# Seven half-size products per part: the next part's transposes and sums in the first half of a part, and two places for those sums

## The chip, the cores and the metric

The kernel runs on one core of a Trainium2 chip. A core has a matrix engine (TensorE, PE in the profile; its weight loads are PEld), a vector engine (VectorE, DVE), an activation engine (ScalarE, ACT), GpSimd (POOL, which here issues the gathers and the adding writes), SyncE (SP, which issues the plain loads) and 16 DMA engines. The metric is device time in microseconds (us). Everything is in float32.

## The reference

A layer of attention and feed-forward is followed by a second one, whose last step is a mixture of experts. The change touches only that step:

```python
routing_weights = softmax(x2d @ gate_kernel)                 # 2048 tokens, 32 experts
routing_weights, selected = top_k(routing_weights, 8)
routing_weights = routing_weights / sum(routing_weights)
w0 = ragged_dot(sorted_inputs, gate_proj, group_sizes)       # 512 -> 192, each row by its expert
w1 = ragged_dot(sorted_inputs, up_proj, group_sizes)         # 512 -> 192
expert_out = ragged_dot(silu(w0) * w1, down_proj, group_sizes)   # 192 -> 512
output = sum over a token's 8 experts of routing_weight * expert_out
```

The tokens are 4 x 512 = 2048, the width is 512, and the hidden width of an expert is 192. The second layer's output is the input plus this sum.

## The kernel before

The experts are ranked by how many rows they got. Rank r has a fixed room of so many tiles of so many rows (`FIXED`: 7 tiles of 126 rows for the fullest, 2 tiles of 100 for the emptiest). `work` holds the 32 ranked experts in the order in which they are computed; an expert with more than four tiles is cut into two **parts** (7 tiles are 3 + 4, 6 are 3 + 3, 5 are 2 + 3), the others are one part. There are 46 parts. The main loop runs over them under a manual schedule: on TensorE, VectorE and ScalarE the instructions stand in the order in which the code issues them. The queues of POOL and SP are filled in the same course, with their own waits.

A part of n rows goes like this. Its gathered rows are transposed (`turn`: four chunks of 128 of the 512 columns; TensorE transposes L1374; three chunks are copied out by ScalarE, L1382, the fourth by VectorE, L1380). The hidden width of 192 is computed as three column groups of 128: gate 0 to 127, up 0 to 127, and one mixed group with the last 64 of gate and of up. The mixed group is a plain product of n columns (L1397), followed by `silu_half` (ScalarE L1198, two VectorE multiplications L1203). The first two groups are done either as plain products (L1397, with L1682 and L1686 after them) or by `Blocks.products` as **seven products of half the columns** (Strassen's scheme in Winograd's form): the weights are four blocks (gate1, gate2, up1, up2, by halves of the 512), the transposed rows four blocks (x11, x12, x21, x22, by halves of the 512 and halves of the rows). Four sums of weight blocks (s1 to s4, `weight_sums`, L1559 to L1562, once per expert) and four of row blocks (t1 to t4, `row_sums`, L1580 to L1584, once per part) are made on VectorE.

The text calls the products of a part, in TensorE's order:

- P1 = gate1·x11, P2 = gate2·x21, P3 = s2·t2, P4 = s1·t1, P5 = s4·x22, P6 = s3·t3, P7 = up2·t4 (all L1598, two matmuls each), and P8, the mixed group (L1397, four matmuls of n columns).

Between them VectorE adds (L1604): P1 + P2 (then SiLU into the low half of sg, L1609), u2 = P1 + P3, u4 = u2 + P4, u4 + P5 (then SiLU into the high half, L1617), u3 = u2 + P6, u3 + P4 (multiplied by sg into the high half of h1, L1621), u3 - P7 (into the low half, L1625). The products alternate between two pools of two PSUM banks each (`bank`); a product waits until the last reader of its bank is done.

`output` of a part is run inside the next part: the downs of a pair of tiles (L1209 and L1212, 512 columns), then the scaling by the routing weight (ScalarE L1485, for the second tile VectorE L1483), then the adding writes on POOL (L1413). A part of three or four tiles has two such groups, a part of two tiles one.

In the kernel before, the order within a part is: P1, P2; first group of downs; P3, P4; transposes of chunk 0 of the next part; P5; second group of downs; P6; chunk 1; P7; chunk 2; then t1 of the next part and, where a new expert follows, s1 to s4; P8 and `silu_half`; chunk 3; t2, t3, t4; the output weights of the next expert (L1440, L1443); the gathers of the expert three ahead (`more`, L916). The sums have one place: ws (s1 to s4) and us (P1, u2 to u4) share the tile big2, ts is in big0. The tiles big1 and big3 are idle in this stage once the early experts' rows, which lay in them, have been added.

The loads of an expert's weights (`fetch`: gu L908, d1 L909, d2 L910) and of its row list (L928) are in SP's queue; each waits until its buffer is free (three buffers).

Of the kernel before, what the change touches and what calls it, by code (L numbers as in the profile page):

```python
# [9 lines left out]
F32 = mybir.dt.float32  # L10
# [8 lines left out]
P = 128  # L19
# [4 lines left out]
EARLY = 6  # L24
# [26 lines left out]
def kernel(  # L51
# [26 lines left out]
    nc = tc.nc  # L78
# [3 lines left out]
    E, MI, _ = w_dn.shape  # L82
# [19 lines left out]
    big = ctx.enter_context(tc.tile_pool(name="big", bufs=1))  # L102
# [1219 lines left out]
    with tc.tile_pool(name="rw", bufs=1, reuse_waits="tile") as rw, tc.tile_pool(  # L1322
# [218 lines left out]
        class Blocks:  # L1541
# [3 lines left out]
            def __init__(self):  # L1545
                ws_us, ts = (
                    big.tile([P, 2048], F32, tag=f"big{i}", name=f"big{i}") for i in (2, 0)
                )
                ws_us = ws_us.rearrange("p (i m) -> p i m", i=8)
                self.ws = [ws_us[:, i, :].rearrange("p (k m) -> p k m", k=2) for i in range(4)]  # L1550
                self.us = [ws_us[:, 4 + i, :] for i in range(4)]
                ts = ts.rearrange("p (i k m) -> p i k m", i=4, k=2)
                self.ts = [ts[:, i, :, :] for i in range(4)]

            def weight_sums(self, gu):
                sub = ALU.subtract
                s1, s2, s3, s4 = self.ws
                gate1, gate2, up1, up2 = self.weights(gu)
                nc.vector.tensor_tensor(s1, up1, up2, ALU.add)  # L1559
                nc.vector.tensor_tensor(s2, s1, gate1, sub)  # L1560
                nc.vector.tensor_tensor(s3, gate1, up1, sub)
                nc.vector.tensor_tensor(s4, gate2, s2, sub)  # L1562

# [11 lines left out]
            def row_sums(self, xgt, n, first):  # L1575
                sub = ALU.subtract
                t1, t2, t3, t4 = (t[:, :, : n // 2] for t in self.ts)
                x11, x12, x21, x22 = self.blocks(xgt, n)
                if first:
                    nc.vector.tensor_tensor(t1, x12, x11, sub)  # L1580
                else:
                    nc.vector.tensor_tensor(t2, x22, t1, sub)
                    nc.vector.tensor_tensor(t3, x22, x12, sub)
                    nc.vector.tensor_tensor(t4, t2, x21, sub)  # L1584

            def products(self, gu, xgt, n, h1, sg, among):
                m = n // 2
                lo, hi = slice(0, m), slice(m, n)
                s1, s2, s3, s4 = self.ws
                t1, t2, t3, t4 = (t[:, :, :m] for t in self.ts)  # L1590
# [4 lines left out]
                def product(w, x):  # L1595
                    q = bank()
                    for k in range(2):
                        nc.tensor.matmul(  # L1598
                            q[:, :m], w[:, k, :], x[:, k, :], start=(k == 0), stop=(k == 1)
                        )  # L1600
                    return q[:, :m]

                def plus(out, a, b, op=ALU.add):
                    nc.vector.tensor_tensor(out, a, b, op)  # L1604

                nc.scalar.copy(p1, product(gate1, x11))
                q = product(gate2, x21)
# [3 lines left out]
                plus(u2, p1, product(s2, t2))  # L1611
                q22 = product(s1, t1)
# [32 lines left out]
        with tc.manual_schedule(engines=order):  # L1645
# [10 lines left out]
            outputs = iter(())  # L1656
            for i, (k, t0, nt) in enumerate(parts):
# [3 lines left out]
                after, todo, nxt = None, iter(()), None  # L1661
# [5 lines left out]
                by_seven = nxt is not None and n_nxt % 2 == 0  # L1667

                def step():
                    return next(todo, None)  # L1670

                places = iter((
                    lambda: next(outputs, None),
                    step,
                    lambda: next(outputs, None),
                    step,
                ))
                if i and n % 2 == 0:
                    seven.products(x.wt[0], xgt, n, h1, sg, lambda: next(places)())
                else:  # L1680
                    p = product(x.wt[0], xgt, 0, n)
                    nc.scalar.activation(sg[:, :n], p[:, :n], AF.Silu)  # L1682
                    next(places)()
                    p = product(x.wt[0], xgt, 1, n)
                    next(places)()
                    nc.vector.tensor_mul(h1[:, :n], p[:, :n], sg[:, :n])  # L1686
                    next(places)()
                    next(places)()
# [186 lines left out]
```

## Time and profile before

| | before |
|---|---|
| time, median of 3 runs | 1727.82 us (1725.8 to 1729.0) |
| the profiled execution | 1772.52 us |
| its span, first to last instruction | 1770.7 us |
| mean granted TensorE clock | 0.98 |
| stage of the ranked experts in it | about 1104 to 1758 us |
| instructions | 19464 |

The profile is of one execution, which took longer than the timed ones; sums are made within it. A line of a group or of the timeline names the source line, the engine, the operation and the tile that is written and those that are read ("g" is a bank of products, "tr" a bank of transposes, "dn" of downs, "xgt" transposed rows, "gu" an expert's gate and up weights, "big" the tiles of the sums). In the timeline the first two columns are start and duration in us; square brackets hold the idle time before an instruction and what ended it. A matmul in float32 appears as two records, so P1 is "x4".

### The profile page before, as it was taken

What the parts mean: (1) busy time and instruction counts of PE and PEld (TensorE: products, weight loads), DVE (VectorE), ACT (ScalarE), POOL (GpSimd) and SP (SyncE); (2) the same over time, 40 slices, a digit from 0 to 9 for tenths busy, and PEclk for the clock granted to TensorE, in tenths of its full rate; (3) what the DMA queues carried; (4) which work ended last, traced back from release to release, by engine and by line L of the source; (5) the groups of instructions that cost most, each with busy time, mean ns of one, the idle gap of its engine ahead of it and who ended that gap; (6) DMA issues with size and microseconds to landing.
All of it is one profiled execution on the core that took longest, in us unless ns stands there. A gap on an engine that the chain in (4) does not pass through costs nothing.

```text
span 1770.7 us, 19464 instructions
## 1 busy us (share of the span) xinstructions
PE 1662.0 (94%) x6530; PEld 1057.1 (60%) x6530; DVE 947.0 (53%) x2273; ACT 556.5 (31%) x993; POOL 600.1 (34%) x522
## 2 busy tenths in 40 slices
PE   7999999999999999999999779898999999999996
PEld 2784667776777677445445346565556666655553
DVE  4683467765775545444334226455255665565653
ACT  2510333322331111265556342232223232232331
POOL 1000130101100100113443646575556655555653
PEclk9999999999999999999999989999999999999998
DMA  9313140000000000722411226787677776687874
GB/s 347 112 60 107 48 175 25 1 1 1 1 0 24 0 1 1 251 101 94 139 51 47 71 89 173 187 157 153 147 165 173 171 152 149 154 176 183 178 151 52
DMA packets 94092, 188.88 MB, mean 107 GB/s; under 512 B 22016, under 2 KB 24704, under 8 KB 93990
## 3 DMA queue, kind: packets, MB, share of 16 engines
q0 software_dynamic: 40560, 74.02, 22.4%
q1 hardware_dynamic: 52564, 112.75, 19.0%
q8 instruction: 52, 0.85, 0.2%
q10 hardware_dynamic: 866, 0.85, 0.2%
q14 instruction: 50, 0.41, 0.1%
HBM read 133.46 MB, written 57.54 MB: 108 GB/s over the span
## 4 chain that ended last, share of the span: by engine, by line
PE 83%; DVE 6%; issue 4%; ACT 3%; DMA 2%; another core or an unknown queue 1%; POOL 0%; ACTq 0%; DVEq 0%; POOLq 0%
PE q L729 16%; PE dn L376 11%; PE g L1598 9%; PE g L1397 7%; PE dn L1209 7%; PE o L1030 6%; PE dn L1212 5%; PE sc L1000 5%; PE gu L354 5%; PE tr L1374 3%; PE g L1253 2%; PE tr L179 2%; DMA out_dram<-y,ids 1%; DVE h L1203 1%; DMA x_sb<-in_cn_dram 1%
## 5 line engine op out<-in xcount | busy, mean ns | idle before, releaser
L1413 POOL DMA_INDIRECT out_dram<-y,ids x141 | 226.1, 1604 | 149.5 <-ACT y L1485 89.2
L376 PE MATMUL dn<-wdn,h 128*128 128x512 f32 x448 | 200.3, 593 | 0.0
L1096 POOL DMA_INDIRECT il_d<-entry,slots x128 | 126.1, 985 | 206.6 <-DVE sel L1064 136.7
L916 POOL DMA_INDIRECT xg<-xn_d,ids x141 | 152.9, 1084 | 119.0 <-issue 60.4
L729 PE MATMUL q<-big,s 128*128 128x256 f32 x768 | 173.6, 379 | 0.0
L729 PEld LDWEIGHTS q<-big,s 128*128 128x128 f32 x768 | 145.9, 190 | 19.8
L1397 PE MATMUL g<-xgt,gu 128*128 128x351 f32 (+24 forms) x464 | 151.6, 470 | 2.2 <-DVE xgt L1380 2.2
L1209 PE MATMUL dn<-d,h 128*126 128x512 f32 (+8 forms) x306 | 148.4, 602 | 0.0
L376 PEld LDWEIGHTS dn<-wdn,h 128*128 128x128 f32 x448 | 84.1, 190 | 92.8 <-issue 91.6
L729 PE MATMUL q<-big,wgu 128*128 128x256 f32 x576 | 132.4, 379 | 0.0
L729 PEld LDWEIGHTS q<-big,wgu 128*128 128x128 f32 x576 | 109.3, 190 | 25.7 <-issue 9.3
L1030 PE MATMUL o<-big,pt 128*128 128x512 f32 x256 | 118.1, 610 | 3.8 <-ACT pt L182 2.0
L354 PE MATMUL gu<-big,wgu 128*128 128x256 f32 x512 | 118.0, 388 | 3.3 <-ACT sg L361 3.3
L1000 PE MATMUL sc<-big,qt 128*128 128x512 f32 x256 | 116.5, 609 | 0.3 <-ACT qt L182 0.3
L354 PEld LDWEIGHTS gu<-big,wgu 128*128 128x128 f32 x512 | 98.6, 194 | 26.6 <-issue 8.7
L1397 PEld LDWEIGHTS g<-xgt,gu 128*128 128x128 f32 x464 | 83.7, 192 | 47.6 <-issue 21.4
L386 POOL TENSOR_TENSOR x_sb<-x_sb,y 128x512 f32<-128x512 f32 x16 | 19.8, 1269 | 258.0 <-DVE y L385 258.0
L1598 PEld LDWEIGHTS g<-big,big 128*128 128x128 f32 x480 | 72.9, 190 | 57.2 <-issue 49.8
L290 POOL TENSOR_TENSOR x_sb<-x_sb,beta_t 128x512 f32<-128x512 f32 x16 | 23.8, 1509 | 236.7 <-ACT y L279 224.2
L1212 PE MATMUL dn<-d,h 64*126 64x512 f32 (+8 forms) x306 | 99.7, 641 | 0.2 <-DVE h L1203 0.2
L743 ACT ACTIVATE sg<-q,wsu_t 128x256 f32<-128x256 f32 x96 | 45.5, 474 | 171.4 <-DVE q L765 84.0
L1485 ACT ACTIVATE y<-dn,w 126x512 f32<-126x512 f32 (+8 forms) x95 | 63.9, 687 | 110.6 <-PE dn L1212 110.6
(273 smaller groups left out, 2560.5 us busy)
## 6 DMA issues: line engine op xcount, KB each, us to landing
gu<-in_w_gu_dram SPq DMA_DIRECT2D x38, 768.0 KB
big<-in_cn_dram SPq DMA_DIRECT2D x10, 1024.0 KB
d<-in_w_dn_dram SPq DMA_DIRECT2D x38, 256.0 KB
big<-in_ct_dram SPq DMA_DIRECT2D x8, 1024.0 KB
x_sb<-in_cn_dram SPq DMA_DIRECT2D x12, 512.0 KB
il_d<-x_sb SPq DMA_DIRECT2D x10, 512.0 KB
d<-in_w_dn_dram SPq DMA_DIRECT2D x38, 128.0 KB
xn_d<-xr SPq DMA_DIRECT2D x16, 272.0 KB
```

Source lines behind the costliest of these rows:

```text
L354: nc.tensor.matmul(ps[:, :n], wt[:, c, fs], xhs[b][:, c, cols], start=(c == 0), stop=(c == DC - 1),)
L376: nc.tensor.matmul(ps[:, :D], h[:, i * P : (i + 1) * P], wdn[:, fc, :], start=(fc == 0), stop=(fc == FC - 1),)
L729: nc.tensor.matmul(q[:, m * HS : (m + 1) * HS], w[:, m, k, :], x[:, k, :], start=(k == 0), stop=(k == 1),)
L916: ins = nc.gpsimd.indirect_dma_start(out=xg, out_offset=None, in_=src[:, :], in_offset=bass.IndirectOffsetOnAxis(ap=idx, axis=0), bounds_c ...
L1000: nc.tensor.matmul(ps[:, bass.ts(h, M // 2)], qt[:, c, :], keys[b][h][:, c, :], start=(c == 0), stop=(c == DC - 1),)
L1030: nc.tensor.matmul(ps[:, :D], pt[:, c, :], values[b][c // (MC // 2)][:, c % (MC // 2), :], start=(c == 0), stop=(c == MC - 1),)
L1096: ins = nc.gpsimd.indirect_dma_start(out=il_d[:, :], out_offset=bass.IndirectOffsetOnAxis(ap=slots[:, j : j + 1], axis=0), in_=entry, in_o ...
L1209: nc.tensor.matmul(p[:q, :D], h1[:, bass.ts(i, q)], d1, start=True, stop=False)
L1212: nc.tensor.matmul(p[:q, :D], h2[half, bass.ts(i, q)], d2[half, :], start=False, stop=True)
L1397: nc.tensor.matmul(p[:, :n], gu[:, c, m * P : (m + 1) * P], xgt[:, c, :n], start=(c == 0), stop=(c == DC - 1),)
L1413: ins = nc.gpsimd.indirect_dma_start(out=of[:, :], out_offset=bass.IndirectOffsetOnAxis(ap=idx, axis=0), in_=y, in_offset=None, bounds_che ...
L1598: nc.tensor.matmul(q[:, :m], w[:, k, :], x[:, k, :], start=(k == 0), stop=(k == 1))
```

## The change

`Blocks` gets two places each for the weight sums (in big2 and big3) and for the row sums (in big0 and big1), and takes them by turns, so the next part's sums can be written while the current ones are read. `row_sums` and `weight_sums` hand back the sums they wrote, and `products` is given them.

Within a part `among()` is called at six places instead of four. After P1: chunk 0 of the next part. After P2: chunk 1, then the first group of downs. After P3: chunk 2. After P4 (`last_turn`): chunk 3, then all four row sums, then the output weights if a new expert follows, then the gathers. After P5 and the adding to it (`next_weights`): the four weight sums if a new expert follows. After P6 and its two addings: the second group of downs. P7 and P8 follow without anything between. After P8 nothing is left of the next part's preparation, and its P1 comes next.

The seven products are now used only from the fourth part on (`i + 1 >= EARLY // 2` for the next part, with EARLY = 6), since the early experts' rows are still in big1 and big3 before that; the second and third part are done with plain products.

```diff
             def weight_sums(self, gu):
-                s1, s2, s3, s4 = self.ws
+                self.rooms_w = self.rooms_w[::-1]
+                s1, s2, s3, s4 = self.rooms_w[1]
...
-            def row_sums(self, xgt, n, first):
+            def row_sums(self, xgt, n):
-                t1, t2, t3, t4 = (t[:, :, : n // 2] for t in self.ts)
+                self.rooms_t = self.rooms_t[::-1]
+                sums = t1, t2, t3, t4 = [t[:, :, : n // 2] for t in self.rooms_t[1]]
                 x11, x12, x21, x22 = self.blocks(xgt, n)
-                if first:
-                    nc.vector.tensor_tensor(t1, x12, x11, sub)
-                else:
-                    nc.vector.tensor_tensor(t2, x22, t1, sub)
-                    nc.vector.tensor_tensor(t3, x22, x12, sub)
-                    nc.vector.tensor_tensor(t4, t2, x21, sub)
+                nc.vector.tensor_tensor(t1, x12, x11, sub)
+                nc.vector.tensor_tensor(t2, x22, t1, sub)
+                nc.vector.tensor_tensor(t3, x22, x12, sub)
+                nc.vector.tensor_tensor(t4, t2, x21, sub)
+                return sums
...
                 nc.scalar.copy(p1, product(gate1, x11))
+                among()
                 q = product(gate2, x21)
...
                 among()
                 plus(u2, p1, product(s2, t2))
+                among()
                 q22 = product(s1, t1)
...
+                seven_next = nxt is not None and n_nxt % 2 == 0 and i + 1 >= EARLY // 2
+
+                def turn_step():
+                    got["xgt"] = next(todo, None)
+
+                def last_turn():
+                    turn_step()
+                    if nxt is None:
+                        return
+                    if seven_next:
+                        got["x"] = seven.row_sums(got["xgt"], n_nxt)
+                    if after[1] == 0:
+                        got["w"] = nxt.weights()
+                    more(*after)
+
+                def next_weights():
+                    if seven_next and (after[1] == 0 or not by_seven):
+                        got["s"] = seven.weight_sums(nxt.wt[0])
+
                 places = iter((
+                    turn_step,
+                    lambda: (turn_step(), next(outputs, None)),
+                    turn_step,
+                    last_turn,
+                    next_weights,
                     lambda: next(outputs, None),
-                    step,
-                    lambda: next(outputs, None),
-                    step,
                 ))
...
-                following = step()
-                if by_seven:
-                    seven.row_sums(following, n_nxt, True)
-                    if after[1] == 0 or not (i and n % 2 == 0):
-                        seven.weight_sums(nxt.wt[0])
                 silu_half(product(x.wt[0], xgt, 2, n), h2, s2, nt, x.q)
-                step()
-                if by_seven:
-                    seven.row_sums(following, n_nxt, False)
                 outputs = output(x, t0, nt, h1, h2, w)
-                xgt = following
-                if nxt is not None:
-                    if after[1] == 0:
-                        w = nxt.weights()
-                    more(*after)
+                of_w, of_x, w, xgt = (got[v] for v in ("s", "x", "w", "xgt"))
```

More of the change, by code (lines that the diff above doesn't have):

```diff
@@ L1545, in __init__, with room, four @@
             def __init__(self):
[L1546 to L1553, printed above, removed]
+                def room(i):
+                    pool = big3 if i == 3 else big
+                    return pool.tile([P, 2048], F32, tag=f"big{i}", name=f"big{i}")
+                def four(v, w):
+                    v = v[:, : 4 * w].rearrange("p (i k m) -> p i k m", i=4, k=2)
+                    return [v[:, i, :, :] for i in range(4)]
+                rooms = [room(i) for i in (2, 0, 1, 3)]
+                self.us = [rooms[0][:, 1024 + i * 256 : 1280 + i * 256] for i in range(4)]
+                self.ws, self.ts = [], []
+                self.rooms_w = [four(rooms[i], 2 * P) for i in (0, 3)]
+                self.rooms_t = [four(rooms[i], 512) for i in (1, 2)]
             def weight_sums(self, gu):
                 sub = ALU.subtract
-                s1, s2, s3, s4 = self.ws
+                self.rooms_w = self.rooms_w[::-1]
+                s1, s2, s3, s4 = self.rooms_w[1]
                 gate1, gate2, up1, up2 = self.weights(gu)
@@ L1562, in weight_sums @@
                 nc.vector.tensor_tensor(s4, gate2, s2, sub)
+                return self.rooms_w[1]
             def weights(self, gu):
@@ L1573, in blocks, with products @@
                 ]
-            def row_sums(self, xgt, n, first):
+            def row_sums(self, xgt, n):
                 sub = ALU.subtract
-                t1, t2, t3, t4 = (t[:, :, : n // 2] for t in self.ts)
+                self.rooms_t = self.rooms_t[::-1]
+                sums = t1, t2, t3, t4 = [t[:, :, : n // 2] for t in self.rooms_t[1]]
                 x11, x12, x21, x22 = self.blocks(xgt, n)
-                if first:
-                    nc.vector.tensor_tensor(t1, x12, x11, sub)
-                else:
[L1582 to L1586, printed above, removed]
+                nc.vector.tensor_tensor(t1, x12, x11, sub)
[3 more added lines that the diff above has]
+                return sums
+            def products(self, gu, xgt, n, sums, h1, sg, among):
                 m = n // 2
                 lo, hi = slice(0, m), slice(m, n)
-                s1, s2, s3, s4 = self.ws
-                t1, t2, t3, t4 = (t[:, :, :m] for t in self.ts)
+                s1, s2, s3, s4, t1, t2, t3, t4 = sums
                 p1, u2, u3, u4 = (u[:, :m] for u in self.us)
@@ L1656 @@
             outputs = iter(())
+            of_w = of_x = None
             for i, (k, t0, nt) in enumerate(parts):
@@ L1660 @@
                 h1, h2, sg, s2 = hidden()
-                after, todo, nxt = None, iter(()), None
+                by_seven = of_x is not None
+                sums = by_seven and of_w + of_x
+                todo, after, nxt = iter(()), None, None
                 if i + 1 < len(parts):
@@ L1666, with among @@
                     n_nxt = after[2] * nxt.q
-                by_seven = nxt is not None and n_nxt % 2 == 0
-                def step():
-                    return next(todo, None)
-                places = iter((
+                seven_next = nxt is not None and n_nxt % 2 == 0 and i + 1 >= EARLY // 2
[13 more added lines that the diff above has]
+                        got["s"] = seven.weight_sums(nxt.wt[0])
+                got = {"s": of_w, "x": None, "w": w, "xgt": None}
+                places = iter((
+                    turn_step,
[3 more added lines that the diff above has]
+                    next_weights,
                     lambda: next(outputs, None),
-                    step,
-                    lambda: next(outputs, None),
-                    step,
-                ))
-                if i and n % 2 == 0:
-                    seven.products(x.wt[0], xgt, n, h1, sg, lambda: next(places)())
+                ))
+                def among():
+                    next(places)()
+                if by_seven:
+                    seven.products(x.wt[0], xgt, n, sums, h1, sg, among)
                 else:
@@ L1682 @@
                     nc.scalar.activation(sg[:, :n], p[:, :n], AF.Silu)
-                    next(places)()
+                    among()
+                    among()
                     p = product(x.wt[0], xgt, 1, n)
-                    next(places)()
                     nc.vector.tensor_mul(h1[:, :n], p[:, :n], sg[:, :n])
-                    next(places)()
-                    next(places)()
+                    for _ in range(4):
+                        among()
                 for _ in outputs:
```

## The prediction

> **What bounds the kernel now.** I read the busy times first, then who waited for whom on TensorE, then one part in order of time, then the granted clock after long waits. The busy line of the page:
>
> ```profile
> PE 1662.0 (94%) x6530; PEld 1057.1 (60%) x6530; DVE 947.0 (53%) x2273; ACT 556.5 (31%) x993; POOL 600.1 (34%) x522
> ```
>
> TensorE (PE) sets the time; VectorE (DVE) is half idle. Work comes off TensorE or a wait of it goes, or nothing is gained. Its waits in the stage of the ranked experts, 1104 to 1758 us (total, times, longest):
>
> ```profile
> PE g L1598 <- DVE xgt L1380: 28.1, 35, 3.1
> ...
> PE g L1598 <- issue: 1.9, 4, 0.5
> PE g L1598 <- DVE h L1203: 0.7, 1, 0.7
> ```
>
> These three are one wait: P2 of a part wants the fourth chunk of its own transposed rows, whose copy (L1380) stands behind the SiLU half (L1203) of the part before. 30.7 us over 40 parts. The longest, 3.1, came after ScalarE had started its SiLU 2 to 3 us late in this execution; its like elsewhere is 0.7. So **28.3 us** can be won.
>
> One part in order of time, with 3x126 rows (halves of 189 columns), the next part being 2x120 rows of another expert:
>
> ```profile
> 1418.38 0.37 PE L1374 MATMUL tr<-ident,xg 120*128 120x120 f32 x2
> ...
> 1418.58 0.35 DVE L1604 TENSOR_TENSOR big<-big,g 128x189 f32<-128x189 f32 x1 [0.29 <-PE g L1598]
> 1418.59 0.81 PE L1598 MATMUL g<-xgt,big 128*128 128x189 f32 x4
> ...
> 1419.23 0.80 PE L1598 MATMUL g<-big,big 128*128 128x189 f32 x4
> ...
> 1420.07 0.35 DVE L1604 TENSOR_TENSOR big<-big,g 128x189 f32<-128x189 f32 x1 [0.28 <-issue]
> ...
> 1421.85 0.40 DVE L1580 TENSOR_TENSOR big<-xgt 128x240 f32<-128x240 f32 x1
> 1422.17 0.42 DVE L1559 TENSOR_TENSOR big<-gu 128x256 f32<-128x256 f32 x1
> 1422.62 0.42 DVE L1560 TENSOR_TENSOR big<-big,gu 128x256 f32<-128x256 f32 x1
> 1422.96 0.42 DVE L1561 TENSOR_TENSOR big<-gu 128x256 f32<-128x256 f32 x1
> ...
> 1423.30 0.42 DVE L1562 TENSOR_TENSOR big<-gu,big 128x256 f32<-128x256 f32 x1
> ...
> 1425.02 0.41 DVE L1380 COPY xgt<-tr 128x240 f32<-128x240 f32 x1
> 1425.46 0.41 DVE L1582 TENSOR_TENSOR big<-xgt,big 128x240 f32<-128x240 f32 x1
> ...
> 1425.48 0.48 PE L1598 MATMUL g<-xgt,gu 128*128 128x120 f32 x2 [0.95 <-DVE xgt L1380]
> ...
> 1425.79 0.40 DVE L1583 TENSOR_TENSOR big<-xgt 128x240 f32<-128x240 f32 x1
> ...
> 1426.10 0.40 DVE L1584 TENSOR_TENSOR big<-big,xgt 128x240 f32<-128x240 f32 x1
> ...
> 1426.42 0.32 DVE L1440 TENSOR_TENSOR w<-xg,hot 120x160 f32<-120x160 f32 x1
> ...
> 1426.78 0.32 DVE L1443 TENSOR_REDUCE w<-w 120x5 f32<-120x160 f32 x1
> 1427.01 0.28 DVE L1604 TENSOR_TENSOR g<-big,g 128x120 f32<-128x120 f32 x1
> ```
>
> The reader should see where the sums lie: four of the weights (1422.17 on) under P8, which runs from 1420.94 for 2.71 us, and three of the rows under the first downs. TensorE waits for none of them.
>
> **What goes.** All 28.3 us: the fourth transposes, their copy and the sums are done well before the next part begins.
>
> **What comes: a chain on VectorE ahead of P8.** VectorE runs its instructions in program order. At the fourth place (between P4 and P5) it now gets the fourth copy, four row sums and the two instructions of the output weights; at the fifth (ahead of P6's adding) four weight sums where a new expert follows. Behind them stands u3 (L1604 after P6), the last reader of P6's bank, and P8 needs a bank. The trace tells which: P8 starts at 1420.94 while L1621, reader of P4's bank, runs from 1420.92 to 1421.27, so P8 doesn't wait for that one; the other bank of the pool is P6's, read by u3. In the kernel before u3 was always early. Now, for the part shown, from the start of its fourth transposes:
>
> - VectorE: u4 starts 0.20 after them (1418.38 to 1418.58) and takes 0.35, so the copy starts at 0.58; copy 0.39 (0.41 long; the next sum may start between 0.08 before its end and 0.04 after, I take 0.02 before); first row sum 0.43 (the second reads it), three more at 0.33 spacing 0.98; weights 0.59 (1426.42 to 1427.01); the adding after P5 0.28; weight sums 0.45 + 3 x 0.34 = 1.47; u3 0.35 and 0.06 to TensorE. Sum 5.13.
> - TensorE: transposes 0.21, P5, P6 and P7 0.64 each (1418.59 to 1419.23). Sum 2.13, as the part before has two tiles and leaves no downs for the sixth place. P8 waits **3.0**.
>
> By the same rows, with 0.55 for a row sum of 378 columns and 0.69 for 504, and the downs that fill the sixth place (2.01 for one tile, 1406.45 to 1408.46; 2.87 for two, 1401.82 to 1404.69), over the 37 parts of seven products that have a next part:
>
> - six with weight sums and no downs there (three-tile ends of five-tile experts): 3.0 each, 18.2
> - eight with weight sums and one tile: for 3x120 before 3x108, 5.41 against 4.17; mean 1.4, 11.1
> - eleven with weight sums and two tiles: for 4x126 before 4x126, 6.66 against 5.84, so 0.8; mean 0.6, 6.8
> - eight with row sums alone and one tile: 3.6 against 3.7, nothing; one with no tile, 1.5
> - three before an odd part, no sums: nothing.
>
> Together **37.6 us**. If each chain is 0.3 shorter it is 28 to 29, if 0.3 longer 48. The spaces above are measured in another order of the same instructions, which is why I allow that much.
>
> **Two parts lose the seven products.** The second and third part now take the plain form: gate and up of 504 columns are two products of 3.38 (P8 of such a part, 1587.98 to 1591.36) against seven of 0.86, +0.7; of 384 columns likewise +0.6. **+1.3.**
>
> **The clock after a 3.0 wait.** Here row and rule disagree. After an idle stretch of 2.78 us that ended at 69.75, in windows of 2 us (columns: stretch, busy times, then granted clock, DMA share, GB/s):
>
> ```profile
> 68.00:70.00 2.00, 0.25 (x1) 0.25 (x2) 0.27 (x1) 1.99 (x3) 0.00 (x0) 1.00 0.00 0
> 70.00:72.00 2.00, 2.00 (x8) 1.63 (x8) 2.00 (x3) 1.35 (x2) 0.00 (x0) 0.69 0.00 0
> 72.00:74.00 2.00, 2.00 (x6) 1.65 (x5) 1.70 (x4) 0.00 (x0) 0.00 (x0) 0.50 0.00 0
> ```
>
> and 0.96 in the next: 2 x (0.31 + 0.50 + 0.04) = 1.7 us lost. Waits of 2.83, 2.91 and 3.06 (ending at 1001.66, 725.64, 1213.97) were followed by 0.64 and 0.50, 0.52 and 0.62, 0.55 and 0.60: about 1.7 each. A wait of 1.43 (1377.53) left the clock at 1.00. The Trainium skill, "TensorE: Matmul & The Clock Gate", section "Why this matters for your kernels", asks for no idle gaps over about 3 us, one idle window (given as 3.4 us) being what halves the clock. By the rule six waits of 3.0 just pass: 0, and the sum is 1738.4. By the rows they pay 6 x 1.7 = **10.2**, and the sum is 1748.6. I take the rows: every wait from 2.2 us on that I looked at was followed by a lower clock.
>
> **Moved at no cost, and what covers it.** Gathers of the expert three ahead now stand on POOL's queue before the adds of the sixth place, which wait up to 4 x 1.38 longer. POOL needs 4 x (1.59 + 0.30) + 4 x (1.08 + 0.30) = 13.1 us in the 17 to 18 us of a four-tile expert, and y has three buffers, so a part more to land; with that cover gone a late add would hold y's writer by up to 5.5 us a part. SP's loads of d1 and d2 wait for the last downs, about 1.3 us later at the sixth place than at the third; they are needed an expert later. The four copies, the transposes and their changes over on TensorE stay as many. The last part has no next one, so nothing is in its way, and the 13 us from TensorE's end (1757.4) to the last add stay.
>
> **Sum.** In the profiled execution 1772.5 - 28.3 + 37.6 + 1.3 + 10.2 = 1793.3. It ran 44.7 us longer than the median of the times, 1727.8; the difference, +20.8, is carried over as it stands: **1748.6 us.**
>
> **Rivals.**
> *The chain is not on TensorE's path.* P8 gets a bank that is read early, or VectorE is through in time. Then the gain stands alone: 1727.8 - 28.3 + 1.3 = 1700.8. For it: VectorE is idle 47% of the span, and its total work falls. Against it: the place; VectorE's idle time lies behind the chain, not in front of it. It decides where the chain is about 1.0 us shorter than worked: waits then sum to 17, the six longest are near 2.1 and leave the clock alone.
> *P8 takes P4's bank.* Then it waits for L1621 too, 0.85 more (1420.42 to 1421.27): waits of about 65 us, clock some 14 us, 1780. Against it: the overlap with L1621 above.
> *Little changes.* The chains are 0.3 to 0.4 shorter, about 28 us, and the clock follows the rule: +1 to +3, about 1730. Four-tile parts speak for it, 0.6 new against 0.65 old.
> *The wait isn't removed.* P2 takes P4's bank and could wait for L1621 at the start of the next part. L1621 ends 0.8 us after P8 starts, and P8 takes 1.62 even at 200 columns: nothing.
>
> **Chances.** The forecast 0.66, its own range 1732 to 1762 (chains 0.3 either way, clock 0 to 12). Chain off the path 0.14; P4's bank 0.08; little change 0.12, of which most lies within 0.2% (3.5 us, about what a measurement of this kernel can tell from no change). So faster 0.16, same 0.10, slower 0.74. The range 1718 to 1768 leaves out most of the first and the second rival.
>
> **What would show it.** Right: L1598 waiting for L1380 is gone; L1397 waits for L1604 in some 26 parts, near 3 us in six, where the clock then falls to about 0.5; L1604 is named as the releaser. Wrong: no wait before L1397 (first rival), L1621 as its releaser (second), or six waits near 3 us and a clock of 1.00 after them.

## The result and the profile after

The changed kernel takes 1734.9 us (median of six runs, 1730.6 to 1739.9) where the kernel before takes 1728.4 (1725.8 to 1730.0): ratio 1.0039, interval 1.002 to 1.0057. It is 6.5 us slower; the forecast was 20.8 us slower, 1748.6. The profiled execution took 1730.6 us with a span of 1728.8.

The busy line and the costliest group of P8 on the page of the changed kernel, then the waits of TensorE in its stage (total, times, longest):

```profile
PE 1648.2 (95%) x6506; PEld 1050.0 (61%) x6506; DVE 930.7 (54%) x2245; ACT 547.4 (32%) x989; POOL 603.2 (35%) x522
...
L1397 PE MATMUL g<-xgt,gu 128*128 128x351 f32 (+24 forms) x496 | 169.0, 487 | 31.0 <-DVE big L1610 31.0
```

```profile
PE g L1397 <- DVE big L1610: 31.0, 25, 2.8
```

The wait of P2 for the fourth chunk (L1380) is gone, all of it. In its place P8 (L1397) waits for the adding u3 (L1610, which was L1604 before), 25 times. That is the wait that the prediction described, at its place and with its releaser. The part of its worked example, 3x126 rows before 2x120 of another expert, looks like this in the timeline of VectorE and TensorE:

```profile
1374.59 0.37 PE L1374 MATMUL tr<-ident,xg 120*128 120x120 f32 x2
1374.79 0.35 DVE L1610 TENSOR_TENSOR big<-big,g 128x189 f32<-128x189 f32 x1 [0.50 <-PE g L1604]
...
1375.06 0.40 DVE L1380 COPY xgt<-tr 128x240 f32<-128x240 f32 x1
1375.37 0.40 DVE L1587 TENSOR_TENSOR big<-xgt 128x240 f32<-128x240 f32 x1
...
1376.92 0.31 DVE L1440 TENSOR_TENSOR w<-xg,hot 120x160 f32<-120x160 f32 x1
...
1377.76 0.42 DVE L1565 TENSOR_TENSOR big<-gu 128x256 f32<-128x256 f32 x1
...
1379.22 0.35 DVE L1610 TENSOR_TENSOR big<-big,g 128x189 f32<-128x189 f32 x1
...
1379.62 1.36 PE L1397 MATMUL g<-xgt,gu 128*128 128x378 f32 x2 [2.74 <-DVE big L1610]
1380.07 0.35 DVE L1629 TENSOR_TENSOR h<-g,sg 128x189 f32<-128x189 f32 x1
```

From the fourth transposes (1374.59) to P8 (1379.62) the chain takes 5.03 us; it was worked out as 5.13. P8 starts before L1629, the reader of P4's bank: the rival that P8 takes P4's bank falls here.

The granted clock around two of the six long waits, in windows of 2 us (the columns are the stretch, its length, the busy times of PE, PEld, DVE, ACT and POOL, then clock, DMA share and GB/s). The first wait ends at 1315.24, the second at 1354.56:

```profile
1314.00:1316.00 2.00, 0.76 (x1) 0.50 (x2) 1.86 (x7) 0.00 (x0) 1.69 (x2) 0.77 0.94 115
1316.00:1318.00 2.00, 2.00 (x5) 1.09 (x4) 0.66 (x3) 0.00 (x0) 1.70 (x2) 0.50 0.91 114
1318.00:1320.00 2.00, 2.00 (x10) 1.35 (x9) 0.00 (x0) 0.26 (x1) 1.39 (x3) 0.88 0.79 228
1354.00:1356.00 2.00, 1.44 (x5) 0.93 (x6) 1.83 (x6) 0.00 (x0) 1.73 (x1) 1.00 0.64 75
1356.00:1358.00 2.00, 2.00 (x13) 1.49 (x12) 0.04 (x2) 0.51 (x2) 1.67 (x2) 1.00 0.77 92
```

The first lost 2 x (0.23 + 0.50 + 0.12) = 1.7 us, the second nothing, though the waits were 2.78 and 2.72. Of the six, three lowered the clock; the side-by-side runs below show which ones do.

So the forecast's mechanism is there, and yet the time rose by a third of what was forecast. The question for the experiments is which term of the sum was mis-sized.

The experiments ran on several chips. On two of them the part of the program ahead of this stage takes some 30 us longer, in both kernels, and the kernel before then takes about 1760 us; each ratio below is against the kernel before on the same chip.

### The profile page after: what moved, and what is told of

Read it like the earlier page. It is cut to its first block, busy times and chain, and to the rows that moved or that the text cites. A ratio compares the mean times of both kernels' runs of the same rounds, so it can differ in the third digit from the quotient of the medians.

```text
span 1728.8 us, 19464 instructions
## 1 busy us (share of the span) xinstructions
PE 1648.2 (95%) x6506; PEld 1050.0 (61%) x6506; DVE 930.7 (54%) x2245; ACT 547.4 (32%) x989; POOL 603.2 (35%) x522
## 5 line engine op out<-in xcount | busy, mean ns | idle before, releaser
L1413 POOL DMA_INDIRECT out_dram<-y,ids x141 | 228.5, 1621 | 207.2 <-issue 64.3
L1397 PE MATMUL g<-xgt,gu 128*128 128x351 f32 (+24 forms) x496 | 169.0, 487 | 31.0 <-DVE big L1610 31.0
L916 POOL DMA_INDIRECT xg<-xn_d,ids x141 | 152.8, 1084 | 44.1 <-issue 33.8
L1397 PEld LDWEIGHTS g<-xgt,gu 128*128 128x128 f32 x496 | 91.6, 194 | 95.2 <-DVE big L1610 38.7
L1209 PE MATMUL dn<-d,h 128*126 128x512 f32 (+8 forms) x306 | 146.0, 593 | 0.0
L1483 DVE TENSOR_SCALAR y<-dn,w 126x512 f32<-126x512 f32 (+8 forms) x46 | 34.5, 751 | 135.4 <-PE dn L1212 114.8
L1485 ACT ACTIVATE y<-dn,w 126x512 f32<-126x512 f32 (+8 forms) x95 | 63.8, 685 | 110.3 <-PE dn L1212 105.5
```

Of the source, the lines that this page charges most:

```text
L916: ins = nc.gpsimd.indirect_dma_start(out=xg, out_offset=None, in_=src[:, :], in_offset=bass.IndirectOffsetOnAxis(ap=idx, axis=0), bounds_c ...
L1209: nc.tensor.matmul(p[:q, :D], h1[:, bass.ts(i, q)], d1, start=True, stop=False)
L1397: nc.tensor.matmul(p[:, :n], gu[:, c, m * P : (m + 1) * P], xgt[:, c, :n], start=(c == 0), stop=(c == DC - 1),)
L1413: ins = nc.gpsimd.indirect_dma_start(out=of[:, :], out_offset=bass.IndirectOffsetOnAxis(ap=idx, axis=0), in_=y, in_offset=None, bounds_che ...
L1485: nc.scalar.activation(y[:q, i, :], p[:q, :D], AF.Copy, scale=weight)
```

## The experiments

**The kernel before and after side by side (c0_before, c0_after).** No edit. The profile shown ahead of the prediction was of an execution of 1772.5 us; this one gives the kernel before without its disturbances.

> The kernel before, unchanged, to have its profile and clock beside the changed kernel's on one chip. Theory (an idle row counts a wait from the modelled end of the last matmul, 0.16 to 0.2 us later than the next one could have started): the stage of the ranked experts lasts 636 to 639 us, about 40 more than in e2_sums_late (597.4), though the rows of waits for L1380, 'issue' and L1203 sum to 30 to 32 only. Rival (the rows count the waits in full): 628 to 632. Time: ratio 0.998 to 1.002.

> The changed kernel, beside the kernel before on one chip. From the two chips so far: 0.9985 to 1.0039 of the kernel before. Theory (P2's wait and P8's wait are worth the same within 3 us, the clock after long waits decides): stage 634 to 639 us, with a lower clock after three to six of the waits, 1.7 us each, and a mean clock 0.003 to 0.005 below that of the kernel before; ratio 0.998 to 1.004. Rival (the prediction's own sizes): +20, ratio 1.012.

Measured: the kernel before 1729.3 us (1724.0 to 1732.6), the changed one 1737.9 (1734.6 to 1746.1), ratio 1.0059 (1.004 to 1.0077); the kernel before against itself 1.0005 (0.9997 to 1.0013). The waits of TensorE in the stage, of the kernel before:

```profile
PE g L1598 <- DVE xgt L1380: 29.0, 40, 1.4
PE tr L1374 <- ACT xgt L1382: 1.1, 4, 0.3
PE dn L1209 <- ACT y L1485: 0.9, 1, 0.9
```

and of the changed kernel:

```profile
PE g L1397 <- DVE big L1610: 33.0, 26, 2.8
PE dn L1209 <- ACT y L1485: 0.8, 2, 0.5
PE tr L1374 <- ACT xgt L1382: 0.3, 1, 0.3
```

Each stage (from its first L1397 to the start of the last L1209) has a length: 1077.5 to 1713.0 = 635.5 before, 1078.9 to 1719.2 = 640.3 after. Up to the P8 of the fourth part they are equal (53.3 and 53.2 us from the stage's first product); from there to the last P8 it is 579.4 and 584.5, **+5.1**. The clock falls after three of the six long waits, 5.1 us in all. The two kinds of wait therefore balance.

The changed kernel's long waits also show the clock without windows, in the durations of the P8 behind them:

```profile
1360.68 4.14 PE L1397 MATMUL g<-xgt,gu 128*128 128x378 f32 x8 [2.72 <-DVE big L1610]
1387.35 2.81 PE L1397 MATMUL g<-xgt,gu 128*128 128x378 f32 x8 [2.66 <-DVE big L1610]
```

The same eight records of 378 columns take 4.14 in one case and 2.81 in the other.

What tells the two cases apart is where the wait falls. In all 14 profiles the granted clock is either 1.00 or 0.50, and it changes only at the steps of a grid of 3.41 us; where the grid begins differs from one execution to the next. Here are the steps that hold the two waits shown for the result's profile, each with the step after it:

```profile
1311.67:1315.08 3.41, 0.79 (x5) 0.50 (x4) 3.34 (x11) 0.33 (x1) 3.06 (x2) 1.00 0.35 28
1315.08:1318.49 3.41, 3.25 (x5) 1.85 (x6) 1.44 (x5) 0.00 (x0) 2.50 (x4) 0.50 0.92 134
...
1352.63:1356.04 3.41, 1.48 (x5) 0.97 (x6) 3.18 (x10) 0.33 (x1) 2.80 (x3) 1.00 0.38 45
1356.04:1359.45 3.41, 3.41 (x21) 2.57 (x20) 1.01 (x3) 1.52 (x5) 2.80 (x3) 1.00 0.82 146
```

The first wait lies almost wholly in one step and leaves TensorE 0.79 us of work in it; the second is split between two steps, and the one shown keeps 1.48. Of the 24 waits of 2.66 to 2.84 us in four profiles (after, c0_after, e0_after, e8_after_gathers_last) 13 lowered the clock, and in each of these TensorE worked at most 1.36 us in one step; the other 11 left it 1.48 or more in every step. Over this stage in all 14 profiles, the 43 steps at full clock with less than 1.4 us of work were all followed by a step at 0.50; of the 2427 with more than 1.6 us one was (1.96 us, in e3_fill below), and of the five between, three.

Over the timed runs the mean clock was 0.991 before and 0.986 after: 0.005 of 1735 is 8 to 9 us, as much as the whole difference in time.

**All sums late (e2_sums_late, c2_sums_late).** The transposes stay early, so P2 has its rows; the row sums, the output weights, the gathers and the weight sums come after P7, so they lie under P8 and no adding stands behind them.

```diff
-                def last_turn():
-                    turn_step()
+                def sums_of_next():
                     if nxt is None:
...
-                    last_turn,
-                    next_weights,
+                    turn_step,
+                    lambda: None,
                     lambda: next(outputs, None),
...
+                sums_of_next()
+                next_weights()
                 silu_half(product(x.wt[0], xgt, 2, n), h2, s2, nt, x.q)
```

> The transposes stay early, all sums and output weights of the next part come after P7's adding, under P8. Theory: no wait before L1397 and none before P2, so the whole gain of the early transposes stands alone. How large it is tells two readings of the old wait apart. Reading one, the idle time of the profile's row (28.3 us): 1728 - 28.3 + 1.3 = 1701. Reading two, from start to start (the row counts idle time only from the modelled end of the last matmul, which lies about 0.16 us behind the point at which the next could start, so 40 parts hide 6.4 more): 1728 - 34.7 + 1.3 = 1695. Rival (the early transposes win nothing by themselves): 1728.

> The kernel of e2_sums_late again, to price the wait that the change removed: transposes early as in the changed kernel, all sums after P7, so that neither P2 nor P8 waits. In c0_before the parts from the fourth on last 579.4 us from P8 to P8 and in e2_sums_late 542.3. Theory (the removed wait is worth 37 us, not the 28 to 29 of its idle row): where the kernel before takes 1729 us, this one takes 1688 to 1693, ratio 0.976 to 0.979; where it takes 1760 with its own clock losses on top, 1714 to 1722, ratio 0.973 to 0.978. Rival (the row has the full size): 1699 to 1702 where the kernel before takes 1729, ratio 0.983 to 0.985.

Measured: 1714.7 us against 1759.9 (ratio 0.9743, 0.9716 to 0.9769), and on another chip 1695.3 against 1728.5 (0.9793, 0.977 to 0.9816). In the first profile TensorE has no wait ahead of P2 or P8. From the fourth part's P8 to the last P8 it takes **542.4 us**, so the kernel before loses 579.4 - 542.4 = **37.0 us** there, and the changed one 42.1. The profiles are from different chips, but in 44 of the 50 steps from one P8 to the next this one and that of the second run agree within 0.01 us. In the second run one down waited 2.3 us for a late y and the clock fell behind it; that part took 18.3 us in place of 13.2. This may be why it came out 2 us above the range that the theory gave.

The idle rows of the kernel before sum to 31 us in the stage, of which P2's wait from the fourth part on is 27.0 (37 times), not 37. One wait shows why. TensorE in a four-tile part of the kernel before, then the same piece of a part with all sums late:

```profile
1531.11 1.44 PE L1598 MATMUL g<-xgt,gu 128*128 128x252 f32 x6
1533.19 0.69 PE L1598 MATMUL g<-xgt,gu 128*128 128x252 f32 x2 [0.64 <-DVE xgt L1380]
1533.72 1.88 PE L1209 MATMUL dn<-d,h 128*128 128x512 f32 x4
```

```profile
1506.71 1.01 PE L1604 MATMUL g<-xgt,gu 128*128 128x252 f32 x4
1507.57 0.60 PE L1374 MATMUL tr<-ident,xg 126*128 126x126 f32 x4
1508.00 1.02 PE L1604 MATMUL g<-xgt,gu 128*128 128x252 f32 x4
1508.85 0.60 PE L1374 MATMUL tr<-ident,xg 126*128 126x126 f32 x4
```

Four such records lead to the next start 0.86 us later (1506.71 to 1507.57), so six take 1.28. In the kernel before the last two should start at 1531.11 + 1.28 = 1532.39 and start at 1533.19: 0.80 late. The row says 0.64, since it counts from the modelled end of the six (1532.55), 0.16 after the point where the next could have started. Over the 37 waits, taken one by one from the starts, that is 6.1 us. The two records behind the wait then lead to the next start 0.53 later (1533.19 to 1533.72), where two of four take 0.43; over the 37 waits that is another 3.7. Together 27.0 + 6.1 + 3.7 = 36.8 of the 37.0.

**Weight sums behind P6's addings (e1_weights_late).**

```diff
-                    next_weights,
-                    lambda: next(outputs, None),
+                    lambda: None,
+                    lambda: (next(outputs, None), next_weights()),
```

> Theory (a chain on VectorE ahead of P8, one instruction after the other): the four weight sums, 1.47 us, leave the chain of every part that a new expert follows. The waits of 2.7 before L1397 become about 1.25, those of 0.9 to 1.6 become 0 to 0.2, those below 0.5 go; in all about 10 us in place of 31.0, and no wait is long enough to lower the clock any more (three were). Time about 21 + 5 us below the changed kernel: 1709 us. Rival (P8 waits for something else, for instance the bank of P4 or the transposes): the waits stay near 31 us and the time near 1735.

Measured: the waits ahead of P8 fall to 10.5 us, as expected. The time hardly falls: 1755.4 against 1759.9, ratio 0.9969 (0.9956 to 0.9982). The last down starts at 1724.2 and the span ends at 1758.9, 34.7 us later; in the changed kernel it was 15.5. The lead is lost on GpSimd. Its queue in the timeline, one expert of four tiles after another (L1413 adds, L916 gathers):

```profile
1610.66 1.60 POOL L1413 DMA_INDIRECT out_dram<-y,ids  x1 [5.11 <-issue]
1612.57 1.59 POOL L1413 DMA_INDIRECT out_dram<-y,ids  x1 [0.30 <-DVE big L1565]
1614.47 1.05 POOL L916 DMA_INDIRECT xg<-xn_d,ids  x1 [0.31 <-issue]
...
1621.71 1.61 POOL L1413 DMA_INDIRECT out_dram<-y,ids  x1 [0.30 <-issue]
1629.72 1.61 POOL L1413 DMA_INDIRECT out_dram<-y,ids  x1 [6.40 <-ACT y L1485]
```

An expert's first add is made, in the code, to wait until the adds of the expert before have landed (they may go to the same rows). Here it starts 8.0 us after the last of them (1621.71 to 1629.72), of which GpSimd is idle for 6.4. The row names a y of ScalarE (L1485), but that one belongs to the pair after it; the y of this add was written by 1621.3, and the last packet of the add before landed at 1628.83, so the landing ended the wait. That idle time lies bare, because the change put the four gathers between the two pairs of adds of one expert. A round takes 19.1 us (1610.66 to 1629.72); TensorE in this kernel needs 16 to 17 for such a part.

**The gathers back at the end of the part (e6_gathers_last, e8_after_gathers_last).** The first starts from e1_weights_late, the second from the changed kernel; both move one call.

```diff
                         got["w"] = nxt.weights()
-                    more(*after)
...
+                if nxt is not None:
+                    more(*after)
                 of_w, of_x, w, xgt = (got[v] for v in ("s", "x", "w", "xgt"))
```

> As e1_weights_late (weight sums behind P6's addings), with the gathers of the expert three ahead put back to the end of the part, where the kernel before has them: on GpSimd's queue they then stand between the adds of two experts instead of between the two pairs of adds of one. Theory: an expert's first add waits until the adds of the expert before have landed, 6.4 us after the last of them was issued; with four gathers (5.4) in between, that time is covered, and GpSimd's round for a four-tile expert goes from 19.5 us to about 18 or less. Then TensorE no longer waits for y (2.8) or for gathered rows (2.3), the end comes 15 to 17 us after the last down instead of 34.7, and the time is 20 to 26 us below the kernel before, ratio 0.985 to 0.989. Rival (the late end of e1_weights_late has another cause than the place of the gathers): the end stays 30 us or more behind the last down, ratio 0.995 to 0.998.

> The changed kernel with the gathers alone put back to the end of the part. Theory (in the changed kernel the adds are just early enough, since TensorE's own waits leave GpSimd the time): no change of the stage, 634 to 639 us, GpSimd's longest idle ahead of an add falls from about 6.5 to 3 or less; ratio as c0_after within 0.002. Rival (late adds already cost the changed kernel something): 3 us or more below c0_after.

Measured: e6_gathers_last takes 1739.0 us, ratio 0.9869 (0.9841 to 0.9898), in the middle of what was expected; its end comes 15.5 us after the last down. The same queue, on the same columns:

```profile
1604.92 1.65 POOL L1413 DMA_INDIRECT out_dram<-y,ids  x1 [3.57 <-ACT sg L1625]
1606.87 1.74 POOL L1413 DMA_INDIRECT out_dram<-y,ids  x1 [0.30 <-DVE big L1567]
...
1611.77 1.07 POOL L916 DMA_INDIRECT xg<-xn_d,ids  x1 [0.30 <-issue]
...
1615.09 1.62 POOL L1413 DMA_INDIRECT out_dram<-y,ids  x1 [0.30 <-ACT y L1485]
1617.02 1.12 POOL L916 DMA_INDIRECT xg<-xn_d,ids  x1 [0.30 <-issue]
1621.35 1.62 POOL L1413 DMA_INDIRECT out_dram<-y,ids  x1 [3.21 <-ACT sg L1625]
```

The round is 16.4 us, where TensorE goes from P8 to P8 in 16.3 to 16.5. So the place of the call was the cause of the late end. How it acts is less simple than expected: on the queue only one of the four gathers came to stand behind an expert's last add, and three are still between its two pairs. GpSimd's idle time falls from 6.4 to 3.2 us; 1.4 of that is the one gather, and 1.7 is that the add before lands 5.5 us after its issue (1615.09 to 1620.55) in place of 7.1. Why it lands sooner is open.

In the changed kernel I expected the same edit to do nothing, and the rival won: 1732.6 us, ratio 1.0019 (1.001 to 1.0028), against 1.0059 (1.004 to 1.0077) for the changed kernel on that chip. By these medians the gathers' place costs the changed kernel about 5 us. What the profiles show of it lies early in the stage, and it is the late add that the prediction had named and put at nothing. VectorE and TensorE of c0_after:

```profile
1156.80 0.75 DVE L1483 TENSOR_SCALAR y<-dn,w 120x512 f32<-120x512 f32 x1 [5.18 <-DMA out_dram<-y,ids]
...
1159.56 0.38 DVE L1590 TENSOR_TENSOR big<-big,xgt 128x224 f32<-128x224 f32 x1
...
1162.35 1.48 PE L1397 MATMUL g<-xgt,gu 128*128 128x360 f32 x4 [1.86 <-DVE big L1610]
```

The scaling of y (L1483) waits 5.2 us for an add that has not landed, because its buffer is still being read by that add. The sums stand behind it on VectorE and u3 behind the sums, so P8 of that part waits 1.86. In e8_after_gathers_last the same scaling waits for TensorE only, and that P8 has a wait of 0.34. The wait of one more part falls from 2.44 to 0.87, and from the stage's first product to the P8 of that part it takes 120.8 us, 3.6 less than the 124.4 of c0_after. The size differs between executions: L1483 waits for an add in three places in c0_after, in one each in the result's profile and e0_after, and in none here.

**Idle matmuls ahead of P8 (e3_fill).** The changed kernel with three matmuls of 384 columns into a bank of transposes that nobody reads, in the parts with the six long waits. It keeps TensorE running while the chain goes on.

```diff
+                if by_seven and seven_next and after[1] == 0 and parts[i - 1][2] == 2:
+                    fill = ps_t.tile([P, 512], F32, tag="tr", name="tr")
+                    for _ in range(3):
+                        nc.tensor.matmul(
+                            fill[:, : 3 * P], ident, x.wt[0][:, 0, :], start=True, stop=True
+                        )
                 silu_half(product(x.wt[0], xgt, 2, n), h2, s2, nt, x.q)
```

> The changed kernel with three matmuls of 384 columns (1.9 us of work whose result nobody reads) between P7 and P8 in the six parts whose wait is 2.7 us. Theory of the clock: the chain ends when it did, P8 starts when it did, but TensorE is idle for about 0.8 us instead of 2.7, so the clock stays at 1.00 there; in the profiled run of the changed kernel three of six waits lowered it at 1.7 us each. Time about 5 us below 1735: 1730, and a narrower spread. Rival (the clock falls for another reason, or the fall costs nothing): the time stays near 1735. If the fillers were in the way instead: up to 6 x 1.9 = 11 us more.

Measured: ratio 0.9975 (0.9959 to 0.999). In the six places the clock now stays at 1.00; it falls once in the stage, elsewhere, behind a wait of 1.64. The stage lasts 631.8 us. The changed kernel in an execution of about that length (e0_after, below) has 637.8, with the clock lowered four times. Three drops fewer are 5.1 of these 6.0 us. The fill doesn't make the chain shorter, so its gain is the clock's share; the two profiles are from different chips, though, and the changed kernel wasn't timed on this one, so the ratios (0.9975 here, 0.9985 for e0_after) can't tell the gain. The mean clock of the timed runs fits this: it is 0.001 below that of the kernel before on this chip, and that of the changed kernel is 0.004 to 0.005 below on its own (e0_after, c0_after).

**One place for the sums, all sums late (e5_one_place_late).** As e2_sums_late with a single place each for weight and row sums, so that seven products run from the second part on.

```diff
-                self.rooms_w = [four(rooms[i], 2 * P) for i in (0, 3)]
-                self.rooms_t = [four(rooms[i], 512) for i in (1, 2)]
+                self.rooms_w = [four(rooms[i], 2 * P) for i in (0,)]
+                self.rooms_t = [four(rooms[i], 512) for i in (1,)]
...
-                seven_next = nxt is not None and n_nxt % 2 == 0 and i + 1 >= EARLY // 2
+                seven_next = nxt is not None and n_nxt % 2 == 0
...
```

> As the run with all sums late, but with one place for the sums, which suffices once they come after P7, and so with the seven products from the second part on as in the kernel before. Theory: no wait before P2 or P8; the 1.3 us of the two plain parts come back. By the start-to-start reading of the old wait 1728 - 34.7 = 1693, by the idle row 1700. If the two places are needed for more than this, a wait of VectorE or TensorE shows up and the time is above that of the run with two places.

Measured: 1723.1 us, ratio 0.9801 (0.9788 to 0.9815); the stage lasts 597.0 us, that of e2_sums_late 597.4. With the sums late, the second places bring nothing in this stage. It ran 8 us longer than e2_sums_late in time; 3 of them lie ahead of the stage in the profiles (it begins at 1103.4 and 1100.3), for the rest I have no reading.

**One place for the sums in the changed order (e4_one_place).** The changed kernel with `rooms_w[:1] * 2` and `rooms_t[:1] * 2` in place of the turns. The next part's sums are then written over t3, t4 and s3 before P6 and P7 are issued, so P6 and P7 multiply the sums of the next part.

> The changed kernel with one place for the sums instead of two, all else as it is. The next part's row sums then have to wait for P6 and P7, which read t3 and t4, while the adding after P5, the weight sums and u3 stand behind them on VectorE. P8 then waits from P7's end for the last row sum 0.33, the output weights 0.59, the adding 0.28, the weight sums 1.47 and u3 0.4, about 3.1 in the 25 parts before a new expert whatever the downs cover, and about 1 in the eleven others: waits of about 88 us in all in place of 31, and 20 to 40 us of clock. Against the kernel before +75 to +100 us, ratio 1.043 to 1.057. Rival (the second places do nothing that the order doesn't do already): as the changed kernel, ratio 1.002 to 1.006.

Measured: ratio 1.0744 (1.0705 to 1.0784) over two executions, more than expected, and with the wait elsewhere:

```profile
PE g L1604 <- DVE big L1567: 96.1, 25, 4.5
PE g L1604 <- DVE big L1589: 14.8, 9, 1.8
```

It is P6 that waits, for the new s3 (L1567), or for the new t3 (L1589). My expectation had the sums wait for P6, which was wrong. The run says nothing on how long correct sums in one place would hold P8, only that this order can't do without a second place.

**The plain parts alone (e7_two_plain).** The kernel before, with seven products from the fourth part on.

```diff
-                by_seven = nxt is not None and n_nxt % 2 == 0
+                by_seven = nxt is not None and n_nxt % 2 == 0 and i + 1 >= EARLY // 2
...
-                if i and n % 2 == 0:
+                if i >= EARLY // 2 and n % 2 == 0:
...
```

> The kernel before with one part of the change alone: seven products only from the fourth part on, so that the second and third part are done with plain products. By the prediction +1.3 us; less the wait for the fourth chunk that these two parts then no longer have ahead of P2, so between 0 and +1.3: ratio 0.999 to 1.002. Rival (the two parts cost more, by the clock or by VectorE): +4 us or more, ratio above 1.0025.

Measured: ratio 0.999 (0.9976 to 1.0005). From the stage's first product to the P8 of the fourth part it takes 53.1 us, the kernel before 53.3. Nothing is lost there.

**The changed kernel on a chip where the kernel before takes 1760 (e0_after).**

> The changed kernel once more, so that it stands on one chip with the runs beside it. Theory (the removed wait is worth 34.7 us from start to start, the new one costs 35, two plain parts 1.3, half of the long waits lower the clock, 5): about +6.5 against the kernel before, ratio 1.002 to 1.006, VectorE's waits ahead of P8 (L1397) about 31 us over some 25 parts, six of them near 2.7, and a clock of 0.50 after two to four of the six. Rival, the prediction's own sizes (every long wait lowers the clock): six of six, and +20.

Measured: 1760.1 against 1762.9, ratio 0.9985 (0.9969 to 1.0). Here the changed kernel isn't slower. Its waits ahead of P8 are 30.3 us, its stage 637.8, much as on the other chips; the mean clock of its runs is 0.979, that of the kernel before 0.983. So the changed kernel loses as much to the clock as elsewhere, and the kernel before must lose more in other ways. The profile shown ahead of the prediction is of such a long execution of the kernel before: its stage lasts 648.1 us, 12.6 more than in c0_before, with a stop of 4.9 us at its beginning, waits of 2.2 and 3.1 in place of 1.4 at most, and three drops of the clock. The profile of e7_two_plain, on the same chip as e0_after and in the order of the kernel before, shows less of it: its stage lasts 638.2, with one wait of 2.15 ahead of a P8 and one drop of the clock. That this happens in the timed runs there is argued from these two profiles, not shown.

## Why the prediction was right in sign and wrong in size

- **The wait that goes: 28.3 us forecast, 37.0 measured from the fourth part on.** This is the step that failed most. The prediction took the idle row of P2's wait as what could be won, and set it against a chain that it worked out from start to start. The row counts from the modelled end of the last matmul, 0.16 us after the next could have started, and leaves out the 0.10 that the records behind the wait lose: 9.8 us over 37 waits. The changed kernel's row is short in the same way (33.0 in c0_after, where the waits cost 37.0). The added wait was charged in full and the removed one was not. Taking off an outlier of 2.4 us, because it came from a late SiLU in one execution, was right: in c0_before the longest wait is 1.4.
- **The chain ahead of P8: 37.6 forecast.** Right in place and releaser, and in size within 5. In e8_after_gathers_last, where the gathers don't disturb it, the stretch lasts 584.0 us, 41.6 more than with all sums late; its clock falls in four places for 8.5, which leaves 33.1. The same count gives 33.4 in the result's profile, 32.7 in e0_after and 37.0 in c0_after. The six long waits were to be 3.0 and are 2.7 to 2.8 by the row, 2.9 from start to start; the worked example was to take 5.13 and took 5.03.
- **The gathers, costed at nothing.** The prediction counted GpSimd's instructions, 13.1 us in 17 to 18, and the longer wait of the adds behind the gathers, saw that a late add would hold y's writer by up to 5.5 us, and concluded that three buffers of y cover it. It left out that an expert's first add waits for the landing of the adds before. One y was held 5.2 us. This costs about 5 us by the medians of c0_after and e8_after_gathers_last, 3.9 by their profiles, and less in the other two profiles of the changed kernel. It also caps what the order could gain without the wait on VectorE: e1_weights_late gave back its lead to it. The first rival, the chain off TensorE's path at 1700.8, left out the same cap.
- **The clock: 10.2 forecast, 5.1 in the two profiles, up to 8 or 9 by the mean clock of the timed runs.** This is the other step that failed. In the profile of before every wait from 2.2 us on that I looked at was followed by a lower clock, and the prediction took the length for the cause; each of them happened to leave TensorE 1.37 us of work or less in one step of the grid (1.37 at the wait of 2.21, 0.35 at 3.06). The Trainium skill, "TensorE: Matmul & The Clock Gate", section "Why this matters for your kernels", speaks of gaps over about 3 us and would have given nothing. Neither holds for 2.7 us: 13 of 24 lowered it, by their place in the grid. As an estimate from these runs: a step keeps less than 1.4 us of work when over 2.0 us of the wait lie in it, and a wait of 2.7 at a random place does that in (3.41 - 2.7 + 2 x 0.7) / 3.41 = 0.6 of all cases. Six times 0.6 times 1.7 is 6, near what was measured.
- **Two plain parts: +1.3 forecast, nothing measured** (e7_two_plain, and 53.3 against 53.2 in the pair). Those two parts also lose their wait ahead of P2, which the sum had counted on the other side. With no such wait in either kernel they do cost 1.4 (51.9 us to the fourth part's P8 in c2_sums_late, 50.5 in e5_one_place_late), so this term was right.

Put right, the sum from the fourth part on is -37.0 + 33.1 + 3.9 + 5.1 = +5.1 for the pair c0. The 3.9 is what is left of the changed kernel's 42.1 and is put down to the gathers, so the sum is an account of the 5.1 and no check of it. The stage grew by 4.8, and the pair of medians differs by 8.6, with the clock's share larger in most timed runs than in the one profiled. For the result's profile, the fastest of its six executions, it is -37.0 + 33.4 + 5.1 = +1.5. What stays open is the sign where the program takes 1760 us.

## What to carry to other kernels

When one wait is traded for another, size both in the same way, from start to start against a part without the wait; an idle row is short by a fixed piece for each wait, and forty small waits make that as large as the answer. For a wait of two to three us, count on the clock falling after some, not all. When a step is moved on a queue, look not only at what the step will delay but at what it had been hiding. Here the early transposes alone, with the sums left under the last product, were worth 33 us (1695.3 against 1728.5), and the changed order gave them back by putting the sums ahead of the last reader of a product's bank, by the clock, and by baring a landing on GpSimd.

## What the runs showed of the hardware that I had not expected

- Whether a wait of TensorE lowers the clock is told by its place in a grid of 3.41 us more than by its length. Of 24 waits of 2.66 to 2.84 us 13 lowered it; the step of the grid then had at most 1.36 us of work, the other 11 had 1.48 or more. Of two waits of 1.86, the one that left 1.55 did so (e0_after) and the one that left 1.68 did not (c0_after); one of 1.64 that left 1.96 did so (e3_fill), against the pattern. Each step at 0.50 costs 1.7 us.
- Three matmuls whose result nobody reads, put into the six long waits, kept the clock at 1.00 there (e3_fill).
- An add that has to follow other adds, since they may go to the same rows, starts 8.0 us after the last of them was issued, with GpSimd idle for 6.4; that last add landed 7.1 us after its issue (e1_weights_late). In e6_gathers_last it landed after 5.5, and with one gather in between the idle time was 3.2.
- The same program takes 1729 us on some chips and 1760 on others, and the changed kernel's ratio was 1.0059 (1.004 to 1.0077) on one of the first and 0.9985 (0.9969 to 1.0) on one of the second.
